# Layer-norm block moves issued from GpSimd instead of SP during a softmax attention

## The chip, the cores and the metric

The kernel runs on one core of a Trainium2 chip. The metric is the device time of the whole kernel in microseconds (us). The core has a tensor engine (TensorE, in profiles PE, with its weight loads as PEld), a vector engine (VectorE, DVE), an activation engine (ScalarE, ACT), GpSimd (POOL) and SyncE (SP). Each engine works through a queue of its own in order, and waits for others through semaphores. DMA transfers are issued from an engine's queue.

## The reference

The input is two sequences of 1,024 rows with 512 features, in fp32. Four blocks follow each other, each on a layer norm of its input and with a residual:

```
x1 = x  + chunked_linear_attention(layernorm(x))
x2 = x1 + ffn(layernorm(x1))                # gate, up, down: 512 -> 1408 -> 512
x3 = x2 + softmax_attention(layernorm(x2))  # one head of width 512
y  = x3 + ffn(layernorm(x3))                # the same weights again

softmax_attention(x): Q, K, V = x Wq, x Wk, x Wv
                      softmax(Q K^T / sqrt(512)) V Wo
```

## The kernel before

The 2,048 rows are 16 tiles of 128 rows; four tiles are a group (ST), and a sequence has two groups, or eight tiles. Every matmul is done in three passes on values split in a high and a low part (`mm3`, lines 96 to 98; `split`, where ACT casts the high part on line 85 and DVE subtracts it on line 86). The instructions are built through a scheduler that lays out each engine's order; `behind(...)` says that some steps come after others.

**The layer norm of a group, transposed.** A matmul needs the normalised rows with features on partitions. For most groups this is not done by TensorE. `ln_norm` loads a tile (line 106), takes its statistics on DVE (lines 108 to 112), raises the variance to -1/2 on GpSimd (`rs`, line 114, one 128x1 instruction), scales on DVE (`xn`, line 116), and has DVE transpose 32x32 blocks into a buffer `y` (line 187). There is one such `y` buffer for all groups. When the four tiles of a group stand in it, `ln_move` brings the blocks to their partitions: four calls (b = 0 to 3) with four DMAs each, so 16 DMAs a group. Each takes 32 partitions of `y` and writes 32 partitions of the slot `xT`, in 16 runs of 32 fp32 values (128 B) per partition, 64 KB in all. The next group's `y` can be written when these 16 have read it.

**The softmax attention** (line 785 on) works on b = 0 and 1, the two sequences. For a tile i of a sequence:

- `scores_b` multiplies the query tile with both groups of keys (`psc`, 24 matmuls), takes the row maximum on DVE (`mx`, line 828; `nm`, lines 831 and 832) and the exponential on ACT (`pe`, line 837).
- `probs_T` transposes `pe`: DVE transposes 32x32 blocks (`py`, line 870), SP stores them to DRAM (line 872), SP loads them back with the blocks in place (`ptl`, four DMAs on line 880), and ACT and DVE split them (`pth` and `ptl`, lines 85 and 86). For the last tile, 15, TensorE transposes instead (`ppt`, line 865), so as not to wait for DRAM.
- `out_b` multiplies with the values (`pob`, 24 matmuls) and adds the residual (line 896).

The order is software-pipelined: TensorE works on the scores of tile i + 1 and then on the output of tile i - 1. Query projections (`pqb`) and value tiles (`pvb`) stand between. All matmuls of this stage are 128x128 by 128x512.

In the same loop two lists of steps (`fill`) run the layer norms that are needed next. Four groups are normalised and moved here, named (nm, st):

| Group | Rows | Needed by |
|---|---|---|
| (b, 2) | x2, tiles 8 to 11 | the second sequence's attention (`ln_split`) |
| (b, 3) | x2, tiles 12 to 15 | the same; scores of tile 8 |
| (g, 0) | x3, tiles 0 to 3 | the second FFN (`combine("g", 0)`: sums and differences on line 244, splits `B_g`, `T_g`) |
| (g, 1) | x3, tiles 4 to 7 | the same |

All DMAs of the kernel, these included, are issued by SP. GpSimd has in this stage only the `rs` instructions.

Of the kernel before, what the change touches and what calls it, by code (L numbers as in the profile page):

```python
# [34 lines left out]
def hybrid_block_kernel(ctx: ExitStack, tc: tile.TileContext, a, out):  # L35
    nc = tc.nc
# [12 lines left out]
    def slot(name, dt=F32R):  # L49

        return wp.tile([P, 2048], dt, tag="slot", name=name)
# [137 lines left out]
    def ln_move(nm, st, b):  # L189

        if b == 0:
            lnT[nm, st] = slot(f"xT_{nm}{st}").rearrange("p (k c) -> p k c", k=KD)
        y = lnY[nm, st]
        xf = lnT[nm, st].bitcast(F32).rearrange("p k (i b q) -> p (k i) b q", i=ST, b=4)
        for c in range(4):
            nc.sync.dma_start(
                out=xf[32 * b : 32 * (b + 1), :, c, :],
                in_=y[32 * c : 32 * (c + 1), b].rearrange("p k i q -> p (k i) q"),
            )
# [12 lines left out]
    def ln_steps(src, nm, st):  # L212

        return [lambda i=i: ln_norm(src, nm, st, i) for i in range(ST)] + [
            lambda b=b: ln_move(nm, st, b) for b in range(4)
        ]
# [804 lines left out]
```

## Time and profile before

| What | Value |
|---|---|
| Median of 3 runs | 1002.87 us (1000.64 to 1003.65) |
| The profiled execution's own time | 1001.88 us |
| Its span, first to last instruction | 1000.2 us |
| Granted TensorE clock, mean | 0.988 |
| Softmax attention in the span | 489 to 775 us |
| TensorE busy in the span | 959.9 us, 96% |
| One move (line 196): time on SP's queue, median | 627 ns |
| One move: issue to landing, median | 2.1 us |
| GpSimd busy from 489 to 775 us | 17.69 us, in 25 instructions |

The profile is one execution, and its times count from the span's first instruction. A row of a timeline gives start, length, engine, line of the kernel, operation, output and inputs, and how many like it were merged; in brackets stands how long the engine was idle before, and what ended that. SPq is the queue from which SP issues DMAs; such a row is the time the queue needed to issue, not the transfer. A matmul's length overlaps with the next one's, so the distance of the starts is the pace.

### The profile page before, as it was taken

What the parts mean: (1) busy time and instruction counts of PE and PEld (TensorE: products, weight loads), DVE (VectorE), ACT (ScalarE), POOL (GpSimd) and SP (SyncE); (2) the same over time, 40 slices, a digit from 0 to 9 for tenths busy, and PEclk for the clock granted to TensorE, in tenths of its full rate; (3) what the DMA queues carried; (4) which work ended last, traced back from release to release, by engine and by line L of the source; (5) the groups of instructions that cost most, each with busy time, mean ns of one, the idle gap of its engine ahead of it and who ended that gap; (6) DMA issues with size and microseconds to landing.
All of it is one profiled execution on the core that took longest, in us unless ns stands there. A gap on an engine that the chain in (4) does not pass through costs nothing.

```text
span 1000.2 us, 13108 instructions
## 1 busy us (share of the span) xinstructions
PE 959.9 (96%) x4450; PEld 789.7 (79%) x4450; DVE 682.6 (68%) x1294; ACT 374.6 (37%) x719; POOL 228.5 (23%) x281
## 2 busy tenths in 40 slices
PE   8999999979898999999999999999988999999998
PEld 6788888867686777887888888888866888788877
DVE  6766858769876699786526556356586675976665
ACT  4653334232665433443222223222133443444421
POOL 4442323253644133212200000000000111321122
PEclk9999999989999999999999999999988999999999
DMA  8636463564698555752704766427768763464113
GB/s 265 204 102 169 126 168 129 153 165 157 234 357 234 143 205 203 185 144 74 262 22 94 167 152 163 101 63 153 168 157 288 250 158 66 151 222 163 38 52 96
DMA packets 250996, 160.08 MB, mean 160 GB/s; under 512 B 187760, under 2 KB 203440, under 8 KB 250928
## 3 DMA queue, kind: packets, MB, share of 16 engines
q1 hardware_dynamic: 250928, 159.23, 54.2%
q8 instruction: 35, 0.57, 0.2%
q14 instruction: 33, 0.27, 0.1%
HBM read 102.66 MB, written 41.84 MB: 144 GB/s over the span
## 4 chain that ended last, share of the span: by engine, by line
PE 52%; DMA 3%; DVE 3%; SPq 2%; ACT 1%; issue 0%; POOL 0%; ACTq 0%; POOLq 0%; DVEq 0%
PE pZg L303 4%; PE pVg L303 4%; PE pXg L303 4%; PE pog L761 4%; PE pog L760 4%; PE pob L96 2%; PE psc L96 2%; PE psc L97 2%; PE pob L97 2%; PE pob L98 2%; PE psc L98 2%; PE pYg L303 2%; PE pof L761 2%; PE pVf L303 2%; PE pof L760 2%; PE pZf L303 2%
## 5 line engine op out<-in xcount | busy, mean ns | idle before, releaser
L761 PE MATMUL pof<-wdf,hsf 128*128 128x512 f32 x176 | 68.4, 392 | 4.5 <-DVE hsf L86 4.5
L761 PE MATMUL pog<-wdg,hsg 128*128 128x512 f32 (+1 forms) x187 | 69.0, 378 | 3.0 <-DVE hsg L86 3.0
L760 PE MATMUL pog<-wdg,hsg 128*128 128x512 f32 (+1 forms) x187 | 69.1, 378 | 0.0
L760 PE MATMUL pof<-wdf,hsf 128*128 128x512 f32 x176 | 68.2, 391 | 0.0
L96 PE MATMUL pob<-vh,pth 128*128 128x512 f32 x128 | 51.8, 405 | 5.7 <-ACT pth L85 5.7
L96 PE MATMUL psc<-xh_b,qh 128*128 128x512 f32 x128 | 51.5, 402 | 0.0
L97 PE MATMUL psc<-xT_b,qh 128*128 128x512 f32 x128 | 51.4, 402 | 0.0
L98 PE MATMUL psc<-xh_b,ql 128*128 128x512 f32 x128 | 51.3, 400 | 0.0
L97 PE MATMUL pob<-vl,pth 128*128 128x512 f32 x128 | 51.2, 400 | 0.0
L303 PE MATMUL pXf<-B_f,wcf 128*128 128x512 f32 x176 | 47.8, 401 | 3.4 <-ACT u2f L728 2.3
L98 PE MATMUL pob<-vh,ptl 128*128 128x512 f32 x128 | 50.8, 398 | 0.0
L303 PE MATMUL pVf<-T_f,wcf 128*128 128x512 f32 x176 | 46.7, 392 | 1.4 <-DVE upf L734 0.7
L303 PE MATMUL pXg<-B_g,wcg 128*128 128x512 f32 x176 | 47.2, 389 | 0.0
L303 PE MATMUL pVg<-T_g,wcg 128*128 128x512 f32 x176 | 46.7, 389 | 0.0
L86 POOL TENSOR_TENSOR hsg<-sgg,hsg 128x128 fp32r<-128x128 f32 x40 | 17.6, 461 | 120.9 <-ACT hsg L85 94.9
L837 ACT ACTIVATE pe<-psc,nm 128x512 f32<-128x512 f32 x32 | 21.7, 683 | 62.7 <-DVE nm L832 62.7
L761 PEld LDWEIGHTS pof<-wdf,hsf 128*128 128x128 f32 x176 | 33.1, 188 | 12.7 <-DVE hsf L86 5.9
L761 PEld LDWEIGHTS pog<-wdg,hsg 128*128 128x128 f32 x187 | 35.1, 188 | 10.0 <-DVE hsg L86 3.6
L303 PEld LDWEIGHTS pXf<-B_f,wcf 128*128 128x128 f32 x176 | 33.0, 191 | 12.7 <-ACT u2f L728 3.9
L85 ACT CAST pth<-ptl 128x512 fp32r<-128x512 f32 x30 | 17.1, 618 | 68.0 <-DMA ptl<-p 57.5
L764 POOL TENSOR_TENSOR xrf<-of,xrf 128x512 f32<-128x512 f32 x16 | 25.0, 1563 | 76.6 <-DVE of L762 54.0
L114 POOL TENSOR_TENSOR rs_g<-ve_g,mhalf 128x1 f32<-128x1 f32 x16 | 10.5, 667 | 139.0 <-DVE ve_g L112 123.7
(286 smaller groups left out, 2642.9 us busy)
## 6 DMA issues: line engine op xcount, KB each, us to landing
wcg<-wc SPq DMA_DIRECT2D x22, 896.0 KB, 4.9
wc<-wcf SPq DMA_DIRECT2D x11, 896.0 KB, 4.4
wcf<-wc SPq DMA_DIRECT2D x11, 896.0 KB, 4.9
p<-py SPq DMA_DIRECT2D x15, 512.0 KB, 3.0
ptl<-p SPq DMA_DIRECT2D x60, 128.0 KB, 3.0
xin_a<-in_x SPq DMA_DIRECT2D x16, 256.0 KB, 4.4
xra<-in_x SPq DMA_DIRECT2D x16, 256.0 KB, 3.0
row<-cl SPq DMA_DIRECT2D x16, 256.0 KB, 4.2
```

Of the source, the lines that this page charges most:

```text
L85: c = nc.scalar.copy(hi, src)
L86: return c.ins, (eng or nc.vector).tensor_tensor(lo, src, hi.bitcast(F32), ALU.subtract).ins
L96: nc.tensor.matmul(ps, lhs_hi, rhs_hi, start=first, stop=False)
L97: nc.tensor.matmul(ps, lhs_hi, rhs_lo, start=False, stop=False)
L98: return nc.tensor.matmul(ps, lhs_lo, rhs_hi, start=False, stop=last).ins
L114: nc.gpsimd.tensor_tensor(rs, ve, mhalf, ALU.pow)
L303: nc.tensor.matmul(ps, w[:, m, k * P : (k + 1) * P], o[:, s, k, :], start=first and k == 0 and s == 0, stop=k == 1 and s == 1, skip_group_ ...
L760: nc.tensor.matmul(ps, hs[i][:, 0, j], wd[j][:, ds], start=j == 0, stop=False)
L761: nc.tensor.matmul(ps, hs[i][:, 1, j], wd[j][:, ds], start=False, stop=j == KH - 1)
L764: add.tensor_tensor(xr[:, ds], o[:, ds], xr[:, ds], ALU.add)
L837: nc.scalar.activation(pe[:, s * 512 : (s + 1) * 512], pS[s], AF.Exp, bias=nm, scale=SC, accum_out=rs[:, s : s + 1],).ins
```

## The change

For the four groups named above, the 16 moves are issued by GpSimd's queue instead of SP's. The groups that are moved in other stages stay on SP. Data, sizes and waits of the moves are the same.

```diff
@@ ln_move(nm, st, b)
         y = lnY[nm, st]
         xf = lnT[nm, st].bitcast(F32).rearrange("p k (i b q) -> p (k i) b q", i=ST, b=4)
+        queue = nc.gpsimd if (nm, st) in (("b", 2), ("b", 3), ("g", 0), ("g", 1)) else nc.sync
         for c in range(4):
-            nc.sync.dma_start(
+            queue.dma_start(
                 out=xf[32 * b : 32 * (b + 1), :, c, :],
                 in_=y[32 * c : 32 * (c + 1), b].rearrange("p k i q -> p (k i) q"),
             )
```

In the changed program each move on GpSimd from the ninth of the first group on also waits for the eighth move before it, as SP's DMAs do in theirs. The scheduler lays out the queues of SP, DVE, ACT and TensorE a little differently from the middle of the first sequence on. On TensorE the matmuls of neighbouring tiles interleave less: the scores of tile 15 come as a whole after the output of tile 12. On DVE the last steps of (g, 1) come later among the splits, and the first two `xn` of the next norm stand ahead of `nm` of tile 14. On ACT the split of (b, 3) stands behind the first value tile's cast.

## The prediction

> **What bounds the kernel now.** I read the page first: TensorE is busy for 96% of the span, so 40 us in all can be won from its idle time, plus what its clock loses.
>
> ```profile
> PE 959.9 (96%) x4450; PEld 789.7 (79%) x4450; DVE 682.6 (68%) x1294; ACT 374.6 (37%) x719; POOL 228.5 (23%) x281
> ```
>
> Then the softmax attention, 489 to 775 us, by stages. Its first 231 us have no idle TensorE at all (columns: stage, length, busy time and count of PE, PEld, DVE, ACT, POOL, granted clock, DMA share, GB/s):
>
> ```profile
> 600.00:640.00 40.00, 40.00 (x176) 32.66 (x176) 22.26 (x45) 12.71 (x26) 1.10 (x2) 1.00 0.66 154
> 680.00:720.00 40.00, 40.00 (x176) 32.71 (x175) 23.48 (x54) 8.25 (x18) 2.88 (x5) 1.00 0.77 163
> 720.00:775.00 55.00, 48.45 (x189) 38.33 (x189) 39.39 (x72) 16.27 (x29) 4.21 (x5) 0.88 0.76 218
> ```
>
> So up to 720 us nothing can be gained, only lost; all the idle time (6.55 us) and the clock of 0.88 are in the last 55 us. TensorE's timeline there shows two gaps, each for a cast of the transposed probabilities (pth, L85):
>
> ```profile
> 734.94 0.79 PE L96 MATMUL pob<-vh,pth 128*128 128x512 f32 x1 [3.43 <-ACT pth L85]
> 735.54 0.63 PE L97 MATMUL pob<-vl,pth 128*128 128x512 f32 x1
> ...
> 758.85 0.80 PE L96 MATMUL pob<-vh,pth 128*128 128x512 f32 x1 [2.29 <-ACT pth L85]
> ```
>
> After each gap matmuls start 0.427 us apart instead of 0.227, for 5 to 6 us (12 or 13 of them): about 2.5 us more per gap. The first gap, out_b of tile 12, is followed back on SP's queue (start, length, line, transfer, count):
>
> ```profile
> 710.75 5.34 SPq L196 DMA_DIRECT2D xT_g<-y_g  x8
> 716.12 0.62 SPq L880 DMA_DIRECT2D ptl<-p  x1
> 716.79 3.96 SPq L196 DMA_DIRECT2D xT_g<-y_g  x6
> 721.10 0.34 SPq L897 DMA_DIRECT2D x<-xrb  x1
> 721.49 1.29 SPq L196 DMA_DIRECT2D xT_g<-y_g  x2
> 722.82 0.62 SPq L872 DMA_DIRECT2D p<-py  x1
> ...
> 726.44 5.39 SPq L880 DMA_DIRECT2D ptl<-p  x4
> ```
>
> DVE finished that p (py, L870) at 716.86; its store left SP at 722.82, 6 us later, behind the 16 moves of (g,1). The four ptl loads, the cast and the gap follow. This is what the change removes. The second gap (tile 14) has no moves in front of it: its py ended at 748.91 and its store left at 749.16.
>
> **What the Trainium skill says.** (1) "DMA: Bandwidth & Descriptors", section "Issuing engines are not separate DMA queues": all issuers share the same 16 DMA engines, and another issuer saves only sequencer time. The trace agrees as far as it goes: the DMA share is 0.68 to 0.77 in the four stretches with moves, so it is SP's time that is short. (2) The same page, section "SWDGE vs HWDGE vs iDMA": a DMA of GpSimd has its descriptors written by software on the Q7 cores, one from SP by hardware; "Latency and other measured facts" gives about 1 us against 0.6 us to the first byte. No run here shows a DMA from GpSimd. (3) "SBUF — State Buffer", section "Who interferes with whom": DVE in a 2-port mode locks GpSimd out. I add nothing for it: DVE's xn (L116) takes 0.55 us for 512 elements, over 1 ns each, with no sign of a faster mode; transposes and subtractions are slower still.
>
> **The change, part by part.** Four groups of 16 moves leave SP and enter POOL's in-order queue: (b,2), (b,3), (g,0), (g,1). Same bytes (64 KB each, runs of 128 B), same waits.
>
> *SP loses* 64 issues of 0.627 us (median of L196's row), 40 us, 10 us in each group. Worth nothing at (b,2), (b,3) and (g,0), since no matmul waited there; at (g,1) it frees the p store of tile 12.
>
> *POOL gains* 64 issues of unknown length c. Bounds: not below SP's 0.627 us, as software won't beat the hardware generator at the same transfer; not above 2.15 us, the price on the page named, section "Anatomy of one DMA — SWDGE (gpsimd) path" (2.0 us + bytes/436e3, which counts the whole DMA as if nothing overlapped). Estimate between: a plain 128-row DMA takes SP 0.32 us (L897 in its timeline at 768.61), a move 0.627, so the many short runs cost 0.31 us more. On the page's 1 us base that is 1.31 us if software adds runs as fast as hardware, and 1.96 us if they scale with the base. I take the middle, **c = 1.65 us**: 26.4 us a group instead of some 11. POOL itself has the room (17.7 us busy of 286), but three things are queued behind the moves: its own rs (L114) of the next tiles, in order; the next block's y transpose on DVE (L187), because y has one buffer; and the splits that read the block. Each then has DVE's or ACT's queue behind it.
>
> I set each group's end (y ready + 16c + 2.1 us to landing) against its next user, in the order in which the changed program's queues are built:
>
> - (b,2): y ready 564.3, landed 592.8. The y of tile 12 is written at 585.1 now and stands on DVE ahead of the second mx of tile 5, then nm, pe, and on ACT pth of tile 4. With 592.8: mx 593.6, pe 596, pth(4) 597.1, ptl(4) 598.7. Its out_b starts at 599.12. Cost 0, with half a microsecond to spare; it begins above c = 1.66.
> - (b,3): y ready 621.2, landed 649.7; split by ACT and DVE from 650.3; scores of tile 8 need it at 651.4. Cost 0, begins near c = 1.7.
> - (g,0): y ready 681.9, landed 710.4. DVE waits there with the y of (g,1). Behind it stand two y transposes, xrb, four bn and mv, rs, two xn, mx of tile 12 and nm: 9.3 us by their rows, so nm(12) at 719.7 (now 713.8). Then pe 721.2, py 722.5, store 3.1, loads 2.4 plus landing, cast: 731.7. But out_b(12) may start at 731.3 at best. So the first gap, 3.43 + 2.5 us, goes almost whole: gain 5 to 6 us at that place.
> - (g,1): y ready about 8 us after 710.4, 718.5; POOL issues until 744.9, landed 747. Behind the moves on POOL is rs of tile 8 of the next norm, and DVE's xn of it stands ahead of nm of tile 14. So nm(14) comes at 746.8; without the wait it would be at 733, psc(14) ending at 731.3. Chain from nm(14): pe 1.6, two ptl splits, the combine's subtraction, two y and a bn with py 4.1, store 3.1, loads and landing 5.1, cast and two T casts 3.3, pe of tile 15 about 1, transposes on TensorE: 19.8 us by rows of the profile. out_b(14) starts at 766.6, now 758.85: **7.7 us late**.
>
> The last item includes the earlier gain, as TensorE then simply waits longer before the last two tiles; the clock dip after that gap is there now too. Sum: +7.7, against the profiled execution's own time of 1001.88 us (span 1000.2): 1009.6. The median of the runs is 1 us above it, 1002.87, so I forecast **1010.5 us**. Edits before the stage: none, at no cost, as the queues are built the same up to tile 3. After it the FFN runs on its own weights, which SP loads no later than TensorE gets there.
>
> By c, the same sums: 0.63 or 1.2 gives nm(14) at 733 and out_b(14) near 753.5, -5 us; 1.45 about +1; 1.65 +7.7. At 2.15 all four groups stall: (b,2) 6.7 + 2.5, (b,3) 7.5 + 2.5, (g,0) moves out_b(12) to about 760, (g,1) out_b(14) to 802: +43 us.
>
> **Rivals.**
>
> *POOL keeps up (faster).* If c is below 1.3, every group lands in time, the first gap closes, and the second stays, since tile 14's chain is the same: -5 us, 998 us, between 996 and 1000. For it: POOL is idle for 94% of the stage; the page calls the generation's share small. Against: 512 runs a move, and hardware already needs twice its plain time for them. Break-even is c = 1.42, by the (g,1) item.
>
> *No gain, no loss.* c from 1.3 to 1.45, where the (g,1) delay eats the closed gap; or the store of tile 12 freed from SP finds another wait (DVE is 72% busy from 720 on, and its order changes there): 1002 us, between 1000 and 1006.
>
> *The moves don't leave SP's bottleneck.* SP's loads of ptl would still be late if the DMA engines, not SP, were short. Against it: shares of 0.68 to 0.77, and landing 2.1 us after issue for 64 KB. 1002 us as well.
>
> **How the numbers follow.** The slow case (c above 1.45) 0.52, of which 0.1 beyond 2.15; keeping up 0.34; no gain, no loss 0.09; SP not the limit 0.05, parted between the sides. 0.3% is 3 us, about what a measurement of this kernel can tell from no change. Faster by over 0.3% 0.35, within 0.12, slower 0.53. The slow case alone spans 1003 to 1045. With the bounds of c at both ends: 996 to 1045.
>
> **What would show it.** In the profile after: POOL's issues of xT_b and xT_g at about 1.65 us each (below 1.3 the forecast falls); no gap at out_b(12) near 731; y_g waiting for xT_g's moves on DVE for about 10 us; xn_g waiting for rs on POOL before nm(14); the gap before the last two out_b grown from 3 to over 10 us; psc of tile 8 not waiting. If there are gaps before 680 us, c is above 1.7 and the time above 1015. If POOL shows moves under 1 us and the time is still not below 1000, the step that is wrong is the (g,1) chain.

## The result, and the profile after

The changed kernel takes 996.67 us (median of 20 runs, 992.68 to 1002.03), the kernel before, run beside it, 1000.31 us (median of 20). The ratio is 0.9964, with a 95% interval of 0.995 to 0.9978: **3.6 us faster**. The forecast was 1010.5 us, 8 us above the median in the table above. The profiled execution took 995.43 us, with a span of 993.7 us and a mean clock of 0.991. Line numbers from 195 on are one higher than before.

The page's first line and the three stretches of the attention (columns as before):

```profile
PE 955.3 (96%) x4450; PEld 786.8 (79%) x4450; DVE 681.8 (69%) x1294; ACT 374.2 (38%) x719; POOL 269.0 (27%) x345
```

```profile
600.00:640.00 40.00, 40.00 (x178) 32.95 (x177) 20.45 (x40) 11.50 (x25) 11.40 (x18) 1.00 0.58 145
680.00:720.00 40.00, 40.00 (x176) 32.72 (x175) 24.09 (x56) 9.52 (x22) 23.22 (x38) 1.00 0.83 193
720.00:775.00 55.00, 48.21 (x206) 39.47 (x205) 39.80 (x70) 18.28 (x31) 3.55 (x5) 0.94 0.75 227
```

POOL now carries the moves. TensorE is still never idle up to 720 us. In the last stretch its busy time is what it was (48.21 against 48.45 us), but its clock is 0.94 instead of 0.88. The idle time has moved, as TensorE's timeline shows:

```profile
728.43 0.39 PE L96 MATMUL pob<-vh,pth 128*128 128x512 f32 x1
...
751.88 1.97 PE L866 MATMUL ppt<-ident,pe 128*128 128x128 f32 x8 [6.79 <-ACT pe L838]
753.50 0.78 PE L96 MATMUL pob<-vh,pth 128*128 128x512 f32 x1
```

The first row is out_b of tile 12: the gap of 3.43 us ahead of it is gone. The two gaps ahead of ppt(15) and out_b(14), 0.82 and 2.29 us before, have become one of 6.79 us. So the sum of idle time is about the same (6.79 against 6.55 us). What is won is a slow stretch: two gaps were each followed by 12 or 13 matmuls at 0.427 us, one gap is followed by some 8. Over all matmuls of the stage (`ppt` left out) that follow each other without idle time, the starts that are more than 0.28 us apart cost 5.9 us over the normal pace before, and 1.7 us after.

SP's queue has the p stores where they belong. Rows of L873 are the stores of tiles 12 and 13, the four loads between are those of tile 12:

```profile
714.41 0.37 SPq L873 DMA_DIRECT2D p<-py  x1
...
720.76 2.87 SPq L881 DMA_DIRECT2D ptl<-p  x4
723.73 0.67 SPq L873 DMA_DIRECT2D p<-py  x1
```

And the disputed price, from the rows of the tiles xT_b and xT_g (shortest, median and longest time in ns, first and last start):

```profile
L197 POOL DMA_DIRECT2D xT_b<-y_b x32: 648/648/850, 562.4 to 628.2; - x32
L197 POOL DMA_DIRECT2D xT_g<-y_g x32: 648/648/684, 679.6 to 718.6; - x32
```

**A move costs POOL 0.648 us, not 1.65**; SP took 0.627. The starts are 0.64 us apart, on SP 0.67. A group of 16 takes 10.3 to 11.5 us; on SP, with other DMAs between, it took 10.8 to 14.7.

From the second query projection of the first sequence to the first matmul of the FFN, the stage has shrunk from 217.6 us (555.07 to 772.62) to 213.7 us (552.40 to 766.08): 3.9 us, about the difference of the medians. The two profiled spans differ by 6.5 us; the rest of it, 2.7 us, lies ahead of the attention. What the attention does before that projection takes 65.3 us in every run, so it is left out, and "stage" with a length below means the stretch from there on. Such a length is of one profiled execution, which in some runs was 2 to 3 us faster or slower than the run's median. Lengths that differ by so little say nothing alone.

### The profile page after: what moved, and what is told of

It is laid out like the page before. It is cut to its first block, busy times and chain, and to the rows that moved or that the text cites. A ratio compares the mean times of both kernels' runs of the same rounds, so it can differ in the third digit from the quotient of the medians.

```text
span 993.7 us, 13137 instructions
## 1 busy us (share of the span) xinstructions
PE 955.3 (96%) x4450; PEld 786.8 (79%) x4450; DVE 681.8 (69%) x1294; ACT 374.2 (38%) x719; POOL 269.0 (27%) x345
## 2 busy tenths in 40 slices
DMA packets 219250, 160.06 MB, mean 161 GB/s; under 512 B 154992, under 2 KB 170672, under 8 KB 219184
## 3 DMA queue, kind: packets, MB, share of 16 engines
q1 hardware_dynamic: 217136, 155.03, 52.3%
## 4 chain that ended last, share of the span: by engine, by line
PE 56%; DVE 2%; SPq 2%; DMA 1%; ACT 1%; issue 1%; POOL 0%; ACTq 0%; DVEq 0%
PE pZg L304 4%; PE pXg L304 4%; PE pVg L304 4%; PE pog L762 4%; PE pog L761 4%; PE psc L96 3%; PE psc L98 3%; PE pob L96 3%; PE psc L97 3%; PE pob L97 3%; PE pob L98 3%; PE pYg L304 2%; PE pof L762 2%; PE pof L761 2%; PE pqb L97 1%; PE pqb L96 1%
## 5 line engine op out<-in xcount | busy, mean ns | idle before, releaser
L765 POOL TENSOR_TENSOR xrg<-og,xrg 128x512 f32<-128x512 f32 x15 | 24.4, 1624 | 61.5 <-DVE og L763 48.7
```

What stands on the lines that cost most here:

```text
L765: add.tensor_tensor(xr[:, ds], o[:, ds], xr[:, ds], ALU.add)
```

## The experiments

All ratios are to the kernel before, run beside each version, with 95% intervals. The expectations speak of theories: T, that only (g,1) on SP ahead of tile 12's store matters; T2 and T3, that the built orders of PE and ACT count too; T4, that the hold-up of DVE at y_g counts. Each later one was formed on the runs made before it.

### Which group's moves matter

```diff
-queue = nc.gpsimd if (nm, st) in (("b", 2), ("b", 3), ("g", 0), ("g", 1)) else nc.sync
+queue = nc.gpsimd if (nm, st) == ("g", 1) else nc.sync
```

> Only the moves of (g,1) are issued by GpSimd; (b,2), (b,3) and (g,0) are on SP as in the kernel before. Theory T (what paid is that the (g,1) moves, some 10 us of SP's issuing, no longer stand ahead of tile 12's p store): all of the change's gain, 3 to 4 us under the kernel before (ratio 0.996 to 0.997), tile 12's store issued right behind its py, and no idle PE at the start of out_b(12). Rival R1 (the gain is the sum of a relieved SP over all four groups): about a quarter of it, 1 us (0.999). Rival R2 (the gain comes from the order in which PE, DVE and ACT were built anew): no relation to the group; anything from 0.995 to 1.003, with a store that is early and a time that doesn't follow.

Measured: 0.9976 (0.9962 to 0.9989), stage 216.4 us. About two thirds of the change's gain at its middle; the intervals overlap, so this run alone can't be told from all of it. The gap ahead of out_b(12) was gone, and 6.55 us stood idle ahead of ppt(15), as in the change.

With the other three groups on GpSimd and (g,1) on SP:

> The moves of (b,2), (b,3) and (g,0) are issued by GpSimd, those of (g,1) stay on SP. T: no gain, within 1 us of the kernel before (0.999 to 1.001), and the idle PE of 3 to 4 us at the start of out_b(12) is back, with the p store of tile 12 issued some 6 us behind its py. R1: three quarters of the gain, -2.7 us (0.997). R2: anything from 0.995 to 1.003.

Measured: **0.9936** (0.9914 to 0.9957), stage 208.9 us. More than the change itself at its middle, where T had expected nothing. T fell here.

Later, two runs took these three groups apart. (g,0) alone:

> Only the 16 moves of (g,0) are issued by GpSimd. The orders of the PE and ACT instructions at the end of the stage then are those of the run that moved (b,2), (b,3) and (g,0). T4 (the change has two sides: moves of a g group that land earlier free the y buffer, of which there is one, so that DVE is not held up at y_g and the exponentials come earlier; and the built order of PE and ACT decides whether that reaches PE): the gain of that run, 5 to 8 us (0.992 to 0.995), with no y_g wait on DVE. Rival T (only (g,1) on SP matters): nothing, 0.999 to 1.001. Rival R1 (relief of SP in proportion): about 1 us, 0.999.

Measured: **0.993** (0.991 to 0.995), stage 210.3 us. At the middles, one group of 16 moves gives about twice what all four give. (b,2) and (b,3) alone:

> Only the 32 moves of (b,2) and (b,3) are issued by GpSimd. The orders of the PE and ACT instructions at the end of the stage are those of the kernel before. T4, T and the prediction alike: PE has no gap before 700 us, so SP's relief there is worth nothing: 0.999 to 1.001, with both y_g waits of DVE and the gap ahead of out_b(12) as before. Rival R1 (relief of SP in proportion): half of the gain, about 2 us (0.998).

Measured: 0.9987 (0.9976 to 0.9998), stage 214.9 us, the gap ahead of out_b(12) still there (2.63 us). About a third of the change's gain at its middle, with an interval that almost reaches 1: some relief that T4 had not expected, and no more. (The profiled execution was 2.4 us faster than this run's median, so its stage looks shorter than the ratio allows.)

### Tile 12's round trip alone

```diff
-nc.sync.dma_start(out=p_d[i]...)                  # and the four loads of ptl
+(nc.gpsimd if t == 12 else nc.sync).dma_start(out=p_d[i]...)
```

> The kernel before, all 64 moves on SP, but the p store of tile 12 and the four loads of ptl(12) are issued by GpSimd (5 issues), so that this one tile's round trip passes the (g,1) moves on SP. T: the place in SP's order is the whole cause, so the gain is that of the change, 3 to 4 us (0.996 to 0.997), and out_b(12) starts without idle PE. Rival R3 (it is the way GpSimd's queue packs the moves into larger packets that pays): the moves are as before, so nothing is gained, 0.999 to 1.001. R1: at most 0.3 us, since 5 of 442 instructions leave SP.

Measured: 1.0012 (0.9997 to 1.0027), nothing gained. The store left at 717.45 us, 5.7 us earlier in the stage than before. But the loads, issued by GpSimd, landed 5.7 us after issue (median; those on SP in the same stretch 3.2):

```profile
717.45 1.10 POOL L873 DMA_DIRECT2D p<-py  x1 [5.15 <-DMA xT_g<-y_g]
722.39 3.12 POOL L881 DMA_DIRECT2D ptl<-p  x4 [3.84 <-DMA xT_g<-y_g]
```

So pth(12) came only 2.5 us earlier, and the idle time went elsewhere: out_b(12) waited 0.81 and 1.85 us in place of 3.43, ppt(15) 3.64 us in place of 0.82. The run tests T with a worse path for the loads, so alone it would not decide; with the two above, T can't stand.

### The order in which PE and ACT were built

A change of a DMA's queue changes the scheduler's plan, and with it the orders of the engines. The kernel before runs 2 matmuls of out_b(12), 11 of scores(15), 22 of out_b(12), the rest of scores(15), out_b(13), ppt(15). The changed kernel runs out_b(12), scores(15), out_b(13), ppt(15) in blocks. The runs with (g,0) but not (g,1) on GpSimd have 2 of out_b(12), all of scores(15), the rest of out_b(12), out_b(13), ppt(15), and on ACT, as the kernel before, pe(15) ahead of pth(14). The next runs set one order at a time, with edges.

The order of the changed kernel on PE, all moves on SP (`behind(...)` the last matmul of out_b(12) around scores(15)):

> All 64 moves on SP as in the kernel before; the one edit puts scores(15) behind the last matmul of out_b(12) on PE, so that PE runs out_b(12), scores(15), out_b(13), ppt(15) in whole blocks, the order that the changed kernel has, instead of the interleaved 2, 11, 22, 13, 24 matmuls of the kernel before. T2 (two things set the tail: when tile 12's p comes back, which SP's queue decides, and how much of PE's work stands between scores(15) and ppt(15), which the built order decides; a version gains only if the two fit): out_b(12) still starts idle by 3 to 4 us, and now nothing of scores(15) has been done meanwhile, so ppt(15) is idle 5 us or more as well: 1 to 5 us over the kernel before (1.001 to 1.005). Rival R2 (the built order alone made the change's gain, not the queue): the gain of the change, 0.996 to 0.997.

Measured: 0.9998 (0.9988 to 1.0009), stage 218.1 us. That order alone wins nothing (R2 fell), and it did no harm either, where T2 had 1 to 5 us.

```diff
-                if i > 0:
-                    out_b(b, i - 1)
+                for n in [i - 1] if b == 0 else [[], [0], [1], [2], [3], [], [4, 5], [6]][i]:
+                    if n >= 0:
+                        out_b(b, n)
```

> All 64 moves on SP as in the kernel before; out_b(12) is written one tile later, behind scores(15), so that PE runs scores(15), out_b(12), out_b(13), ppt(15). T2: the 5.6 us of scores(15) cover what tile 12's p is late, and 48 matmuls (10.9 us) instead of 24 cover the way from scores(15) to pe(15), so both gaps go though no move has left SP; the idle time left is that ahead of out_b(14), 2 to 3 us: 6 to 9 us under the kernel before (0.991 to 0.994), as in the run that left only (g,1) on SP. Rival T (SP's queue is the cause, whatever PE's order): tile 12's p is as late as before and nothing is gained, 0.999 to 1.001.

Measured: 1.0 (0.9988 to 1.0012), stage 219.1 us. T2 missed: the gap was not covered, it moved to out_b(14), 8.49 us.

> The changed kernel with out_b(12) written behind scores(15) as in the run with the same edit and all moves on SP. T2: with the cover in place GpSimd adds nothing more that PE can use, so it lands within 2 us of the version with the moves on SP: 0.990 to 0.994 of the kernel before. Rival T: the early p of tile 12 stays worth its 3 to 4 us, so this one is 3 to 4 us faster than its twin on SP.

Measured: 0.996 (0.9944 to 0.9976), stage 214.8 us, 4 us below its twin on SP. PE's order doesn't replace the change of queue. Why it adds nothing to it shows in ACT's timeline, and below it in PE's:

```profile
753.15 1.14 ACT L85 CAST pth<-ptl 128x512 fp32r<-128x512 f32 x2 [9.08 <-DMA ptl<-p]
754.20 1.99 ACT L85 CAST T_g<-xT_g 128x1024 fp32r<-128x1024 f32 x2
756.09 0.68 ACT L838 ACTIVATE pe<-psc,nm 128x512 f32<-128x512 f32 x1
```

```profile
756.91 1.97 PE L866 MATMUL ppt<-ident,pe 128*128 128x128 f32 x8 [8.51 <-ACT pe L838]
```

ACT runs in order. It stood 9.08 us at the cast pth(14), for loads from DRAM, while pe(15), whose scores were done at 737, stood behind it with two T_g casts between. The changed kernel has the same order there (pth(14) at 748.12, pe(15) at 751.06). The kernel before does not; there pe(15) goes first:

```profile
754.42 0.68 ACT L837 ACTIVATE pe<-psc,nm 128x512 f32<-128x512 f32 x1
...
758.18 1.14 ACT L85 CAST pth<-ptl 128x512 fp32r<-128x512 f32 x2 [1.40 <-DMA ptl<-p]
```

Two edges take it away, and put pe(14) ahead of pth(13) as well:

```diff
-            for s in range(2):
-                ks = slice(s * 4, s * 4 + 4)
-                split(hi[:, ks], lo[:, ks], raw[:, ks])
+            with behind(last[:1] if t in (13, 14) else []):   # the exponential of tile t + 1
+                for s in range(2):
+                    ks = slice(s * 4, s * 4 + 4)
+                    split(hi[:, ks], lo[:, ks], raw[:, ks])
```

First for tile 14 alone:

> The changed kernel with one edge added: on ACT the casts pth(14), which wait for tile 14's loads, are put behind pe(15), in whose way they stood. T3 (what is left of the change's first gap is spent again because ACT and DVE run in order: casts that wait for loads stand ahead of the exponentials that PE's next transposes need): pe(15) starts when its nm and the two T_g casts are done, at 748 to 750 us instead of 751.06, and the idle PE ahead of ppt(15) falls from 6.8 to 4 to 6 us: 1 to 3 us under the changed kernel, 0.993 to 0.996 of the kernel before. Rival R5 (the tail is bound by tile 14's round trip or by DVE's backlog, not by ACT's order): the wait only moves to out_b(14), 0.996 to 0.998.

Measured: 0.9957 (0.9942 to 0.9973), stage 211.8 us; the idle time ahead of ppt(15) fell from 6.79 to 4.61 us, as expected. Then for both tiles:

> The changed kernel with two edges on ACT: pth(13) behind pe(14), and pth(14) behind pe(15). T3: pe(14) starts when nm(14) is there (730.4) instead of behind the loads of tile 13 (735.2), so tile 14's round trip begins some 4 to 5 us earlier, DVE's backlog with it, and pe(15) is in time: idle PE ahead of ppt(15) and out_b(14) of 1 to 3 us in all instead of 6.8: 4 to 6 us under the changed kernel, 0.990 to 0.993 of the kernel before. Rival R5 (DVE's backlog): at most 1 us is gained, 0.995 to 0.998.

Measured: 0.9943 (0.9923 to 0.9963), stage 209.3 us: the stage as expected, the ratio somewhat above. Its PE timeline has three small gaps left, and no slow stretch behind them (clock 1.00 from 720 to 775 us):

```profile
749.82 1.32 PE L866 MATMUL ppt<-ident,pe 128*128 128x128 f32 x8 [1.78 <-ACT pe L838]
...
752.95 0.50 PE L96 MATMUL pob<-vh,pth 128*128 128x512 f32 x1 [1.22 <-ACT pth L85]
...
754.58 0.50 PE L98 MATMUL pob<-vh,ptl 128*128 128x512 f32 x1 [0.90 <-DVE ptl L86]
```

The same edges with all moves on SP, then on GpSimd together with scores(15) first, then all three edits on SP:

> All 64 moves on SP as in the kernel before, with the same two edges on ACT. T3 with T: the first gap, ahead of out_b(12), stays with its slow clock behind it (3.4 us), and ahead of ppt(15) there were only 0.8 and ahead of out_b(14) 2.3 us to be had: within 2 us of the kernel before, 0.998 to 1.000. Rival R6 (ACT's order is all that matters in this tail, and the queue of the moves nothing): as fast as the changed kernel with the same edges, 0.990 to 0.993.

Measured: 0.9987 (0.9969 to 1.0005), the gap ahead of out_b(12) now 4.24 us.

> The changed kernel with the two edges on ACT and with scores(15) ahead of out_b(12) on PE. T3: the run with scores(15) first was idle 8.5 us ahead of ppt(15) because pe(15) stood behind pth(14) on ACT; with that gone, 48 matmuls of out_b(12) and out_b(13) (10.9 us) cover the way to pe(15), and little or nothing is idle but 1 to 2 us ahead of out_b(14): 0.988 to 0.992 of the kernel before. Rival R5 (DVE's backlog): the gap stays over 5 us, 0.994 to 0.997.

Measured: 0.9937 (0.9912 to 0.9961), stage 210.7 us, less than expected; two gaps of 1.76 and 1.06 us are left.

> All 64 moves on SP, with the three edits of order together: scores(15) ahead of out_b(12) on PE, pth(13) behind pe(14) and pth(14) behind pe(15) on ACT. T4: y_g still holds DVE up twice by some 3 us and tile 12's p still comes late, so no order makes up for it wholly: 0 to 3 us under the kernel before (0.997 to 1.000). Rival R7 (the built order is the whole of it, and where the moves are issued does nothing): as the changed kernel with the same edits, 0.992 to 0.995.

Measured: 0.9971 (0.9959 to 0.9984), stage 214.7 us. At their middles the two sides add up, as far as ratios that were measured at different times can be set against each other: all three edits of order are worth 2.9 us on SP (from 1 to 0.9971) and 2.7 us on GpSimd (from 0.9964 to 0.9937); the queue is worth 3.6 us with the built orders and 3.4 us with these. Each of these ratios is uncertain by 1.3 to 2.5 us to either side, PE's built order differs a little between the two (on SP ppt(15) comes earlier), and on SP one of the edits, pth(14) behind pe(15), changes nothing. So the change's gain does not come from the orders that these edits set. They set those of PE and ACT at the end of the stage; the orders of SP and DVE, which the change altered too, were not taken apart from the queue.

Another way around the wait of tile 14 is to transpose it on TensorE too (`if t >= NT - 2`):

> The changed kernel, with tile 14's p also transposed on TensorE, as tile 15's is, in place of its round trip through memory. T: pth(14) no longer waits for the loads (landed at about 748 us in the changed kernel), so ACT reaches pe(15) when its scores are ready instead of behind pth(14); the 6.8 us of idle PE ahead of ppt(15) shrink to 2 to 4 us, against 8 more transposes at the clock of the tail (about 2 us): 1 to 3 us under the changed kernel, 0.993 to 0.996 of the kernel before. Rival R4 (pe(15) is late because of the order on ACT, whatever tile 14 does): no gain, or 1 to 2 us lost to the 8 transposes, 0.996 to 0.998 of the kernel before.

Measured: 0.994 (0.9917 to 0.9963), stage 213.7 us. The gap fell only to 5.23 us, and the stage's length doesn't show what the ratio shows: not settled.

### The hold-up of DVE at y_g

In the kernel before DVE waited twice, 5.8 us in all, to write y_g, since there is one y buffer and the moves of the group before hadn't landed. In the changed kernel both waits are gone. Here (g,1) has a y buffer of its own, all moves stay on SP, and the orders of PE and ACT are those of the kernel before:

```diff
-            lnY[nm, st] = yp.tile(...)
+            lnY[nm, st] = ypool.get((nm, st), yp).tile(...)   # ypool: a pool of its own for ("g", 1)
```

> All 64 moves on SP, y of (g,1) in a buffer of its own, so that its first transposes don't wait for the moves of (g,0) to land, nor the next y_g for those of (g,1). The orders of PE and ACT at the end of the stage are those of the kernel before. T4 (the hold-up at y_g is what the moves on SP cost): both y_g waits of DVE (5.8 us) are gone, (g,1)'s moves are on SP 3 us earlier, so tile 12's p store too, and the gap ahead of out_b(12) shrinks from 3.4 us to under 1: 2 to 4 us under the kernel before (0.996 to 0.998). Rival R8 (SP's time is the cost, and DVE's hold-up is hidden): 0.999 to 1.001, the gap as before.

Measured: 0.9991 (0.9977 to 1.0006), stage 218.0 us. Both y_g waits were gone and the gap stayed:

```profile
738.00 0.50 PE L96 MATMUL pob<-vh,pth 128*128 128x512 f32 x1 [2.89 <-ACT pth L85]
```

But the moves of (g,1) did not come 3 us earlier. They began 158.0 us into the stage, 155.7 before: SP's order has them behind the first three loads of tile 11. So the run doesn't show what earlier moves would bring.

> All 64 moves on SP, y of (g,1) in a buffer of its own, and the three edits of order on PE and ACT (scores(15) ahead of out_b(12), pth(13) behind pe(14), pth(14) behind pe(15)). T4: the two sides of the change without the change: 4 to 7 us under the kernel before (0.993 to 0.996). Rival R8 (SP's time is the cost): no more than the same orders gained with one y buffer, 0.996 to 0.998.

Measured: 0.9965 (0.9952 to 0.9978), stage 213.3 us, within the noise of the same orders with one y buffer (0.9971). T4 fell as far as y goes: to take the hold-up away, and nothing else, gains nothing that can be seen.

### What an issue on GpSimd costs

Each move cut into four, each with four of the 16 runs of a partition, so 64 issues a group:

> The changed kernel with each move on GpSimd cut into four of four 128-byte runs a partition (64 issues a group of the same 256 KB in all). If an issue on GpSimd costs the same whatever it moves (0.65 us, theory C1), a group takes 41 us of POOL in place of 10.3, c is 2.6 us for a quarter of a block, and by the sums of the prediction (43 us lost at 2.15) (g,1) is not in place for pe's scale of tile 14 and (b,2) and (b,3) come late for the scores of tile 0: 40 to 90 us slower than the kernel before (1.04 to 1.09). If the cost follows the runs or bytes (theory C2), an issue takes 0.2 to 0.3 us, a group some 13 to 18 us, and the time is that of the changed kernel within 3 us (0.995 to 1.001).

Measured: **1.0704** (1.0687 to 1.0721), 71 us slower. The tile's row and PE's waits in the stage:

```profile
L199 POOL DMA_DIRECT2D xT_g<-y_g x128: 548/551/583, 705.6 to 823.1; - x128
```

```profile
PE pXg L303 <- DMA wcg<-wc: 59.3, 1, 59.3
PE psc L96 <- ACT xh_b L85: 17.3, 1, 17.3
PE pqb L96 <- ACT xh_b L85: 3.3, 1, 3.3
```

A quarter of a move costs 0.551 us, a whole one 0.648. So 384 runs of 128 B more cost 0.097 us, 0.25 ns each. As an estimate from these two points, if the cost grows in proportion, the 512 runs of a move are 0.13 us, and 0.52 us is fixed; C1 nearly holds. At 4 x 0.551 = 2.2 us for a move's worth POOL can't keep up: the scores of tile 8 wait for (b,3), and the FFN waits for (g,1), whose last move is issued at 823 us. (The FFN's wait is put down to its weights, which came last. In the kernel before SP held loads of these weights 2.6 us for the combine of line 244.)

With the rows of y padded to 36 elements, so that the source is in 512 pieces as well:

> The changed kernel with rows of y padded from 32 to 36 elements (the moves read 32 of them), so that a partition's 16 runs of 128 bytes are apart in the source as well, where they were one run of 2 KB. C1 (the price of an issue is mostly fixed): 0.65 us again, and the time of the changed kernel, 0.995 to 0.998. Rival C2 (the price follows the pieces that have to be described, which were 32 of 2 KB and now are 512 of 128 bytes): over 1 us an issue, 512 packets a move instead of 32, and by the sums of the prediction a time at or over that of the kernel before.

Measured: 0.9971 (0.9959 to 0.9983); 0.648 to 0.651 us an issue, and still 32 packets a move. C1 held, C2 fell.

## Why the prediction was wrong

**The failed step is c.** The text took "1.65 us" for what a move costs GpSimd's queue, and 0.648 us was measured. It came from a base of 1 us and an addition for the many runs between 0.31 and 0.96 us. Both terms were too large: by the estimate above the fixed part is 0.52 us and the runs add 0.13. The base was a time to the first byte, which is latency; what fills a queue is the time an issue holds the engine. The addition was scaled from SP's 0.31 us for short runs, more than twice what the runs add on GpSimd. The lower bound, SP's 0.627 us, was nearly the answer; by the distance of the starts GpSimd is even a little quicker (0.64 us against 0.67). The Trainium skill, "DMA: Bandwidth & Descriptors", section "Anatomy of one DMA — SWDGE (gpsimd) path", says of descriptor generation that it is small and that many can be emitted before the cost shows. The runs agree (0.097 us for 384 runs); the prediction quoted this for the rival and then set it aside. The forecast of slower rested on this one number: its own rival for c below 1.3 gave -5 us, and -3.6 was measured. That these two lie so near is in part luck. The rival counted a closed first gap and an unchanged second one. The traces show 3.4 us of closed gap and 4.2 us less of slow pace, and against them 3.7 us more of idle time ahead of ppt(15) and out_b(14); and part of the gain is that of (g,0), to which the text gave nothing.

**The sums by c** came out too low where POOL is too slow. The text gave +43 us at 2.15; cut in four, 2.2 us cost 71 us. The stall of (b,3) was there (17.3 us of PE, where the text had 7.5 and a slow clock). The (g,1) delay came at the start of the FFN (59.3 us), not at out_b(14). That the queues were planned anew for this run may be why; it is not shown. One sum has a slip: by the times given for (b,2), 598.7 against 599.12, its stall at 2.15 would be 7.6 us, not 6.7; nothing at 1.65 rests on it. The break-even of 1.42 was not tried.

**"At (g,1) it frees the p store of tile 12"** was right: the store leaves 5.8 us earlier in the stage (162.0 against 167.8 us from its start), and the gap at out_b(12) is closed. **"Worth nothing at (b,2), (b,3) and (g,0), since no matmul waited there"** was wrong for (g,0), which alone gives 0.993, and a little for (b,2) and (b,3), 0.9987. With the right c this error would hardly have shown in the number. SP's queue in the kernel before, earlier than I had looked:

```profile
684.15 6.18 SPq L196 DMA_DIRECT2D xT_g<-y_g  x8
690.43 0.56 SPq L897 DMA_DIRECT2D x<-xrb  x1
691.03 5.33 SPq L196 DMA_DIRECT2D xT_g<-y_g  x8
696.47 2.70 SPq L880 DMA_DIRECT2D ptl<-p  x4
699.26 1.18 SPq L106 DMA_DIRECT2D xin_g<-x  x2
700.53 0.39 SPq L872 DMA_DIRECT2D p<-py  x1
...
707.18 0.32 SPq L106 DMA_DIRECT2D xin_g<-x  x1
707.61 2.42 SPq L880 DMA_DIRECT2D ptl<-p  x3
```

and with (g,0) alone on GpSimd:

```profile
689.14 3.55 SPq L881 DMA_DIRECT2D ptl<-p  x4
...
693.55 0.39 SPq L873 DMA_DIRECT2D p<-py  x1
...
702.82 1.53 SPq L881 DMA_DIRECT2D ptl<-p  x3
...
705.54 0.43 SPq L881 DMA_DIRECT2D ptl<-p  x1
```

py(11) was ready at 693.5 us in the kernel before; its store left at 700.53, behind the 16 moves of (g,0) and the loads of tile 10 that they had delayed. Its own loads came at 707.61. The store had landed at 705.26, but SP stood until 707.18 at a load of `xin_g`, whose buffer DVE's `xn_g` had yet to read. The fourth load left at 716.12, behind eight moves of (g,1) (in the lines shown in the prediction). With (g,0) on GpSimd, the first three loads leave 3.7 us earlier in the stage and the fourth 9.5 us, since the order that is then built for SP has it ahead of the moves of (g,1). No run takes that order apart from the queue. No matmul waits for this, so PE's waits don't show it. DVE does (kernel before):

```profile
719.72 0.69 DVE L86 TENSOR_TENSOR ptl<-ptl,pth 128x512 fp32r<-128x512 f32 x1 [2.82 <-ACT pth L85]
...
724.69 0.71 DVE L187 STREAM_TRANSPOSE y_g<-xn_g 128x512 f32<-128x512 f32 x1 [2.42 <-DMA xT_g<-y_g]
725.33 0.65 DVE L828 TENSOR_REDUCE mx<-psc 128x1 f32<-128x512 f32 x1
726.01 0.16 DVE L831 TENSOR_TENSOR nm<-mx 128x1 f32<-128x1 f32 x1
```

The low part of tile 11 stands ahead of mx and nm of tile 13, whose scores were complete at 720.3. Between the two halves of mx(13) stands the y_g of the next norm, idle 2.42 us for the moves of (g,1), and this wait is the last before nm(13). In the run with y apart it is gone, and pe(13) comes only 0.7 us earlier in the stage, with pth(11) 2.4 us later: there the low part of tile 11 holds it. So both are in the way, and no run takes the late tile 11 away and leaves the wait for y. With both, pe(13) is late, and the round trips of the last tiles after it. The steps in each run, in us from the start of the stage (start of each instruction in the ACT and SP timelines, less the start of the second query projection):

| Moves on GpSimd | p(11) stored | pth(11) | pe(13) | p(12) stored | pe(15) | stage | ratio |
|---|---|---|---|---|---|---|---|
| none (before) | 145.5 | 164.0 | 171.4 | 167.8 | 199.3 | 217.6 | 1 |
| none, y apart | 147.1 | 166.4 | 170.7 | 170.2 | 200.4 | 218.0 | 0.9991 |
| none, three edits of order | 145.2 | 165.1 | 172.4 | 168.8 | 191.9 | 214.7 | 0.9971 |
| (b,2), (b,3) | 144.8 | 164.4 | 171.8 | 168.1 | 197.5 | 214.9 | 0.9987 |
| (g,1) | 148.3 | 162.7 | 169.7 | 167.1 | 200.9 | 216.4 | 0.9976 |
| all four (the change) | 138.7 | 154.7 | 166.4 | 162.0 | 198.7 | 213.7 | 0.9964 |
| all four, two edges on ACT | 138.1 | 154.7 | 166.3 | 161.6 | 193.6 | 209.3 | 0.9943 |
| (g,0) | 139.6 | 155.5 | 166.7 | 167.7 | 187.2 | 210.3 | 0.993 |
| (b,2), (b,3), (g,0) | 138.7 | 155.6 | 166.4 | 168.4 | 187.4 | 208.9 | 0.9936 |

Wherever (g,0) has left SP, p(11) is stored 6 to 7 us earlier, pth(11) comes 9 us earlier and pe(13) 5 us earlier, whatever else differs among these runs; (g,1) moves p(12)'s store, and only when (g,0) is gone by the full 6 us. The column pe(15) says what is made of it: in the change it stays at 198.7, with the two edges on ACT it comes at 193.6, and in the runs with (g,0) and not (g,1) at 187. So moving (g,1) as well takes a part of (g,0)'s gain back at the middles of the ratios. The edges, which change nothing on GpSimd, bring most of it back, so the order that the scheduler then builds has a part in it. What holds pe(15) for the other 6 us was not tried; DVE's order differs too.

What is shown: that (g,0) alone pays, that (g,1) alone pays too and at its middle a third as much, that taking the hold-up at y_g away alone doesn't, that the edited orders of PE and ACT are not the change's gain, and the times in the table. What is argued from the traces only is the link from p(11) to pe(13), and how much of it is SP's time and how much the order that is built for SP and DVE. A run that leaves (g,0) on SP and gets only tile 10's loads and tile 11's store past it would show it; it wasn't tried.

**"and the second stays"** (the rival that came true) was wrong: with the small one ahead of ppt(15) it grew from 3.1 to 6.8 us. That is why the gain isn't the 5 us of the closed gap and its slow clock.

**The signs named** came out thus: no gap at out_b(12), no gap before 680 us and scores of tile 8 not waiting, as forecast; the gap before the last two out_b grew from 3.1 us to 6.8, not to over 10; issues of 0.65 us, no y_g waits and no late nm(14), as in the rival. The last clause, that with moves under 1 us and a time not below 1000 the (g,1) chain would be wrong, did not apply.

**Versions that beat both kernels**: (g,0) alone (0.993), all groups but (g,1) (0.9936), and the change with the two edges (0.9943) or with all three edits (0.9937). Against the changed kernel's 0.9964 the intervals overlap or touch, so by how much they beat it is open; the first needs the smallest edit.

## What to carry to other kernels

Before costing a transfer's move to another queue, ask what one issue holds the engine for, not what it takes to the first byte, and when no row shows it, let the issue cost and not a latency carry the range. A queue's relief is not worth nothing where no matmul waits: follow what was behind it (here one store, 7 us late) through the in-order queues of the other engines to the end of the stage. And a changed queue is a changed plan: compare the built orders around each wait, since casts that wait for DRAM ahead of an exponential cost the changed kernel some 2 us at the middle of the ratios (from 0.9964 to 0.9943), where the change brought 3.6.

## What was not expected of the hardware

- GpSimd issues a move of 512 runs of 128 B in 0.648 us, where SP takes 0.627, and starts the next after 0.64 us, SP after 0.67; 128 runs take 0.551 us. Padding the source so that its runs are apart changed nothing.
- Its queue records 32 packets of 2 KB for a move, one for each partition; on SP the same move made 528 (SP's queue has 33,792 fewer for the 64 moves): as many as its 512 runs of 128 B, and 16 more. The page of the changed kernel (packets, MB, share):

```profile
q0 software_dynamic: 2048, 4.20, 2.0%
```

  The kernel's packets fell from 250,996 to 219,250 with it. That this makes the transfers lighter was not seen: they took 2.0% of the DMA engines' time, and SP's share fell by 1.9 (54.2 to 52.3%). Moves on GpSimd landed later, 4.4 us after issue (median, from 700 to 770 us) against 2.1 us on SP. The section "Issuing engines are not separate DMA queues" of "DMA: Bandwidth & Descriptors" in the Trainium skill has it that another issuer saves only sequencer time; these numbers agree.
- What a gap costs in clock isn't read off its length. Two runs whose gaps were 1.1 and 2.4 us, or 1.8, 1.2 and 0.9 us, kept a clock of 1.00 from 720 to 775 us; one with gaps of 0.4 and 2.5 us fell to 0.97, one with 1.8 and 1.1 us to 0.94. The text's 2.5 us a gap held for the two gaps it was read from, not for all.
